# A four-layer convolution network on one core: layer 3's two row differences in one operation, on rows kept in blocks

## The chip, the cores and the metric

The kernel runs on one core of one Trainium2 chip. The metric is device time in microseconds (us) for one execution. The median of three runs of the kernel before is 2742.17 us (2739.24 to 2742.29).

## The reference

The input x is 16 images of 64 channels with 128 x 128 pixels, fp32. Four layers follow each other; each adds to x a function of the group-normalized x (`_gn`: 32 groups of 2 channels).

```
x = x + L0(gn(x))     # Gram matrix of the channels (64x64), applied to the image, then a 1x1 convolution
x = x + L1(gn(x))     # |Sobel x| + |Sobel y|, per channel
x = x + L2(gn(x))     # shift of a quarter of the channels to the left and of a quarter to the right, 3x3 convolution, bias
x = x + L3(gn(x))     # 3x3 convolution with w_bin, 1x1 convolution, batch norm over all images, leaky ReLU, clip to 0..255
```

Layer 3's batch normalization needs sums over all 16 images, so its result can only be finished and added to x when the last image is through.

## The kernel before

**Tiles.** 128 partitions hold 64 channels twice. An image is cut into chunks of R = 8 rows for each of the two sets of partitions, so NS = 8 chunks an image and 128 in all. One chunk of a tile is 128 partitions by 8 x 128 = 1024 elements. CP = 4 is half of the rows of a chunk.

**Order.** One loop over steps, with four quarters q = 0..3 in each, writes the whole order out by hand, for every engine; instructions of an engine stay in program order. In each quarter the stages are called in this order: parts of Front (layers 0 and 1) marked "first of", then Layer3, Layer2, Front, then Layer2's parts marked "last of 0" and "last of 3", then Gram (the Gram matrix of a later image), and then `tick()`, which advances the chains of small operations that make normalization coefficients. Front, Layer2 and Layer3 start at steps 15, 25 and 35, so for the most part a step works on one chunk of layer 1 of an image, one of layer 2 and one of layer 3 of earlier images. When the last chunk of one image and the first of the next meet in a stage, the step is called an image boundary here.

**A convolution by differences.** For two neighbouring output rows (even and odd), the 3x3 products are formed from one product that both share, on the odd rows (`shared`, into the PSUM tile `one`), and one of its own for each (`own`, into the halves of the PSUM tile `two`), on differences of rows: `difference(name, n, t)` (line 703) writes `diffs[name][:, n]`, with n = 0 for even minus odd row and n = 1 for the following even row minus odd row. The tile is `d3` for layer 3 and `d2` for layer 2. `twin(n)` copies a difference once more with its partition halves arranged differently, into qd; for layer 3 with two ScalarE copies, for layer 2 with two DMAs of GpSimd's queue. `own` needs the difference and its twin.

**Layer 3, chunk by chunk** (`Layer3.at`, line 955):

- q 0: twin(1) of the chunk; the shared product; the own product n = 0.
- q 1: the own product n = 1; ScalarE copies `one` with a bias into c; `prepare(i + 1)` (line 928) normalizes the next chunk's rows into a tile v3 of R + 1 = 9 rows in image order: one row from the chunk before, the four odd rows, the four even rows after them (line 942 and 944, in two ScalarE operations whose target takes every second row).
- q 2: VectorE adds `two` and c into y and sums it, which awaits the own products; then the next chunk's difference n = 0.
- q 3: twin(0) of the next chunk; its difference n = 1; ScalarE squares y and sums it.

**Layer 2** in q 0 adds the contributions of the two end columns of the image to the PSUM tile `two`, with one VectorE operation for the left and one for the right column (line 842), then forms x3 = two + c with its sum; then the difference n = 0 of `d2` follows and its twin; in "last of 3" the difference n = 1 and its twin. GpSimd scales the end columns of layer 2's v ahead of that (`keep0`, `keep1`, line 879).

**Front** puts most of VectorE's work: two operations in "first of 0", four in q 1, one in q 2 (called the gx product here, output u from xh) and one in q 3. In q 2 it stands behind layer 3's work on VectorE.

**The end.** Once the batch norm's coefficients are known, every part of y and of x3 is loaded back from memory, combined and stored as output; free tiles of all pools are used as buffers for that (`rest`, line 1033), those of v3 among them.

Of the kernel before, what the change touches and what calls it, by code (L numbers as in the profile page):

```python
# [10 lines left out]
F32 = mybir.dt.float32  # L11
# [5 lines left out]
P = 128  # L17
# [3 lines left out]
R = 8  # L21
NS = HH // R
EARLY = 3
CP = 4
# [84 lines left out]
def tile_kernel(ctx: ExitStack, tc: tile.TileContext, x, cw_h, w2_t, b2, wbin_t, w1_t, b1, gamma, beta, consts, out):  # L109
# [81 lines left out]

    wb = ring.tile([P, (R + 1) * W + 2], F32, tag="v2", name="wb", bufs=3)
    wb = wb[0:C, 0:9 * C].rearrange("p (y x c) -> p y x c", y=3, x=3)
    w1 = ring.tile([P, R + 1, W], F32, tag="v3", name="w1")[0:C, 0, 0:C]

    sp.dma_start(kc[:, 0:P], consts[:, 0:P])
    pool.dma_start(kc[:, P:K_END], consts[:, P:K_END])
# [499 lines left out]


    def by_parity(t):
        v = t[:, 0:R, :].rearrange("p (j s) w -> p s j w", s=2)  # L700
        return v[:, 0], v[:, 1]

    def difference(name, n, t, m=CP):


        even, odd = by_parity(t)
        after = t[:, 1:R + 1, :].rearrange("p (j s) w -> p s j w", s=2)[:, 1]
        dve.tensor_sub(diffs[name][:, n, 0:m, 1:1 + W], (after if n else even)[:, 0:m], odd[:, 0:m])

    def taps(o, p, wts, srcs, pad=0):  # L710

# [53 lines left out]
    class Layer2:  # L765
# [65 lines left out]
        def at(self, i, q):  # L831
            b = self.b
            closing = i + 1 == NS
            m = CP - 1 if closing else CP
            if q == 0:
                if i == NS:
                    chains.append(coefficients(self.st, self.done))
                if 1 <= i:
                    two = self.p.pop(i - 1)[0]

                    e = self.edges.pop(i - 1).rearrange("p t (m n) -> p t n m", n=2)
                    for side, w in ((0, 0), (1, W - 1)):
                        dve.tensor_add(two[:, :, :, w], two[:, :, :, w], e[:, side])
                    x3 = ring.tile([P, 2, CP, W], F32, tag="x3", name=f"x3_{b}_{i - 1}", bufs=NS + 2)
                    tiles3[b].append(x3)
                    dve.scalar_tensor_tensor(
                        x3.rearrange("p s j w -> p s (j w)"), two.rearrange("p s j w -> p s (j w)"), 1.0,
                        self.c.unsqueeze(1).to_broadcast([P, 2, CP * W]),
                        op0=ALU.mult, op1=ALU.add, accum_out=self.st[:, 0, i - 1:i],
                    )  # L850
                if 0 <= i < NS:
                    difference("d2", 0, self.v[i], m)
                    self.twin(0)
            if q == 1:
                if i == 0:

                    self.wi = stp.tile([P, 2, 3, P], F32, tag="wi", name=f"wi_{b}", bufs=1)
                    for n, base in ((0, w2[:, 2]), (1, wm)):
                        dve.scalar_tensor_tensor(
                            self.wi[:, n].rearrange("p k o -> p (k o)"), k("I3"), self.co[:, 2:3],  # L860
                            base.rearrange("p k o -> p (k o)"), op0=ALU.mult, op1=ALU.add,
                        )
                if -1 <= i < NS - 1:
                    if i == -1:
                        self.co = coefs2.pop(b)
                    t, f = self.v[i + 1], self.whole.pop(i + 1)
                    act.activation(f, f, AF.Identity, bias=self.co[:, 1:2], scale=self.co[:, 0:1])


                    e = stp.tile([P, 2, R], F32, tag="edges", name=f"edges_{b}_{i + 1}", bufs=3)  # L870
                    for side, at in ((0, 0), (1, W + 1)):
                        for rows, j in ((lo, 1), (hi, 0)):
                            n = at + j * W
                            pool.tensor_scalar_mul(
                                e[rows, side], f[rows, n:n + (R - 1) * W + 1:W], self.co[rows, 3 + side:4 + side]
                            )
                    self.edges[i + 1] = e

                    pool.tensor_scalar_mul(t[:, :, 0], t[:, :, 0], k("keep0"))
                    pool.tensor_scalar_mul(t[:, :, W - 1], t[:, :, W - 1], k("keep1"))  # L880
                if i + 2 < NS:
                    self.load(i + 2)
            if q == 2:
                if 0 <= i < NS:
                    t = self.v[i]
                    one = ps_one.tile([P, CP, W], F32, tag="one", name=f"one2_{b}_{i}")
                    two = ps_two.tile([P, 2, CP, W], F32, tag="two", name=f"two2_{b}_{i}")
                    self.p[i] = two, one
                    shared(one, self.wi[:, 0], t, m)
                    if closing:  # L890
                        small_product(one[:, m, :], w0, t[:, R, :])

                    both = self.wi[:, 1]
                    own(two[:, 1], 1, TO_SLOTS, w2, "d2", m, both)
                    if closing:

                        p = two[:, 1, m:CP]
                        issue([taps(0, p, [both], [t[:, R:R + 1, :]]), taps(1, p, [both], [t[:, R - 1:R, :]])])

                    self.c = ring.tile([P, CP * W], F32, tag="c2", name=f"c2_{b}_{i}", bufs=1)  # L900
                    act.activation(self.c, flat(one), AF.Identity, bias=self.co[:, 5:6])
                if 1 <= i < NS:
                    self.square(i - 1)
                if 1 <= i:
                    self.store(i - 1)
            if q == 3:
                if 0 <= i < NS:
                    t = self.v.pop(i)
                    two, one = self.p[i]
                    both = self.wi[:, 1]  # L910
                    own(two[:, 0], 0, TO_SLOTS, w2, "d2", m, both)
                    if closing:
                        p, srcs = two[:, 0, m:CP], [t[:, R - 2:R - 1, :], t[:, R - 1:R, :]]
                        issue([taps(0, p, [w2[:, 0], both], srcs), taps(1, p, [both, w2[:, 1]], srcs)])
            if q == "last of 0" and i == NS:
                self.square(i - 1)
            if q == "last of 3" and -1 <= i < NS - 1:
                difference("d2", 1, self.v[i + 1], CP if i + 2 < NS else CP - 1)
                self.twin(1)


    class Layer3:
# [4 lines left out]

        def prepare(self, i):
            b, tiles = self.b, tiles3[self.b]
            t = ring.tile([P, R + 1, W], F32, tag="v3", name=f"v3_{b}_{i}")  # L930
            self.v[i] = t

            def norm(dst, src, co):
                act.activation(dst, src, AF.Identity, bias=co[:, 1:2], scale=co[:, 0:1])

            if i == 0:
                self.co, self.edge = coefs3.pop(b)
                norm(t[:, 0, :], tiles[NS - 1][:, 1, CP - 1, :], self.edge["lower"])
            else:
                norm(t[:, 0, :], tiles[i - 1][:, 1, CP - 1, :], self.co)  # L940
            v = t[:, 1:R + 1, :].rearrange("p (n s) w -> p s n w", s=2)
            norm(v[:, 0], tiles[i][:, 0], self.co)
            m = CP if i + 1 < NS else CP - 1
            norm(v[:, 1, 0:m], tiles[i][:, 1, 0:m], self.co)
            if m < CP:
                norm(t[:, R, :], tiles[i][:, 1, m, :], self.edge["upper"])

        def twin(self, n):

# [5 lines left out]
        def at(self, i, q):  # L955
# [25 lines left out]
            if q == 2:  # L981
                if 0 <= i < NS:
                    y = ring.tile([P, 2, CP, W], F32, tag="y", name=f"y_{b}_{i}")
                    self.y[i] = y
                    two = self.p.pop(i)[0].rearrange("p s j w -> p s (j w)")
                    dve.scalar_tensor_tensor(
                        y.rearrange("p s j w -> p s (j w)"), two, 1.0,
                        self.c.unsqueeze(1).to_broadcast([P, 2, CP * W]),
                        op0=ALU.mult, op1=ALU.add, accum_out=bn_sum[:, n:n + 1],
                    )  # L990
                if i + 1 < NS:
                    difference("d3", 0, self.v[i + 1])
            if q == 3:
                if i + 1 < NS:
                    self.twin(0)
                    difference("d3", 1, self.v[i + 1])
                if 0 <= i < NS:
                    act.activation(
                        junk, self.y[i].rearrange("p s j w -> p (s j w)"), AF.Square,
                        accum_out=bn_sq[:, n:n + 1],  # L1000
                    )
# [104 lines left out]
        tick()  # L1106
    rest(ring, "x3", [2, CP, W], NS + 2, NS + 2 - 3 - (NS - 3))
    rest(ring, "y", [2, CP, W], 2)
    rest(ring, "v3", [R + 1, W], 2)
    while len(room) > 1:  # L1110
        fetch()

# [74 lines left out]
```

## Time and profile before

| | us |
|---|---|
| median of 3 runs | 2742.17 |
| the profiled execution, its own time | 2739.81 |
| its span, first to last instruction | 2738.0 |
| first y of layer 3 | 323.16 |
| last y of layer 3 | 2285.55 |
| last matmul of the network, about | 2285 |

The page gives busy time by engine, 40 slices of the span, and groups of instructions. Up to 300 us the pipeline fills; from there to 2050 all three layers run beside each other; to 2220 layers 2 and 3, to 2285 layer 3 alone; the rest is loading, finishing and storing. The mean granted TensorE clock is 0.899 over the span, and 1.00 in each stretch from 600 to 2250. Matmul ends are modelled, so that TensorE's idle time is better read from the distance of the starts of its instructions than from its busy share. All operations carry line 73, a helper that records the order, so groups are told apart by tile and shape.

### The profile page before, as it was taken

To read this page: it belongs to the slowest core of one execution; us is meant where nothing else is said; L and a number is where in the kernel's file an instruction comes from. 1 tells how busy PE (TensorE), PEld (TensorE's weight loads), DVE (VectorE), ACT (ScalarE), POOL (GpSimd) and SP (SyncE) were. 2 spreads that over 40 slices of the span, in tenths; PEclk is the share of its full clock that TensorE was granted. 3 is DMA by queue.
4 is the path that set the end of the run, shared out by engine and by line. 5 is a ranking of instruction groups with operands and counts; after the bars stand their busy time and mean duration, and the time that the engine had idled before them with its cause. 6 is when DMAs were issued, how large, how long until landed. Compare 5 with 4: busy or idle time off the path is not lost. (4 is left out here: it accounts for less than half of the span.)

```text
span 2738.0 us, 45982 instructions
## 1 busy us (share of the span) xinstructions
PE 2168.3 (79%) x14804; PEld 910.8 (33%) x14804; DVE 2190.3 (80%) x3623; ACT 2108.3 (77%) x3177; POOL 851.7 (31%) x1350
## 2 busy tenths in 40 slices
PE   6578899999999999999999999999999993000000
PEld 4234433434343434343434343333334641000000
DVE  4999999999999999999999999999996335333332
ACT  4766889898989898989899989898997677333332
POOL 2044424442434243333343434445444300000000
PEclk8689999999999999999999999999999997555555
DMA  8799878898888888888889787888887868999999
GB/s 209 200 232 235 224 198 238 217 240 220 236 231 234 226 228 226 228 224 234 224 226 239 211 201 201 204 211 207 220 204 187 226 188 308 419 420 420 420 420 385
DMA packets 693600, 685.95 MB, mean 251 GB/s; under 512 B 60096, under 2 KB 580448, under 8 KB 693360
## 3 DMA queue, kind: packets, MB, share of 16 engines
q1 hardware_dynamic: 668208, 613.83, 76.2%
q0 software_dynamic: 25152, 69.18, 10.0%
q8 instruction: 119, 1.95, 0.3%
q14 instruction: 121, 0.99, 0.1%
HBM read 346.23 MB, written 268.44 MB: 224 GB/s over the span
## 5 line engine op out<-in xcount | busy, mean ns | idle before, releaser
L73 PE MATMUL two<-d,w 128*64 128x508 f32 (+2 forms) x2560 | 855.5, 587 | 0.0
L73 PE MATMUL two<-d,wi 128*64 128x508 f32 (+3 forms) x1536 | 576.1, 578 | 0.0
L73 PE MATMUL two<-qd,pk 128*64 128x512 f32 (+1 forms) x1024 | 521.0, 590 | 27.9 <-DMA qd<-d 19.8
L73 POOL DMA_DIRECT2D qd<-d x512 | 270.8, 531 | 862.4 <-DVE d L73 284.5
L73 POOL TENSOR_SCALAR edges<-v,co 64x8 f32<-64x8 f32 x512 | 334.9, 654 | 352.5 <-ACT v L73 183.8
L73 DVE TENSOR_TENSOR d<-v 128x512 f32<-128x512 f32 (+1 forms) x512 | 346.0, 678 | 58.1 <-issue 30.8
L73 PEld LDWEIGHTS two<-d,w 128*64 128x64 f32 x2560 | 273.0, 136 | 325.1 <-issue 282.1
L73 PE MATMUL one<-v,w 128*64 128x508 f32 (+2 forms) x1600 | 364.6, 579 | 0.0
L73 PE MATMUL one<-v,wi 128*64 128x508 f32 (+3 forms) x1536 | 353.3, 591 | 2.5 <-issue 1.7
L73 ACT COPY qd<-d 64x512 f32<-64x512 f32 x512 | 315.5, 616 | 18.2 <-DVE d L73 12.2
L73 DVE SCALAR_TENSOR_TENSOR e<-e 128x1032 f32<-128x1032 f32 (+1 forms) x256 | 313.0, 1223 | 0.0
L73 ACT ACTIVATE xh<-po,co 128x128 f32<-128x128 f32 (+1 forms) x480 | 275.4, 623 | 26.1 <-PE po L73 22.4
L73 PEld LDWEIGHTS two<-d,wi 128*64 128x64 f32 x1536 | 178.8, 136 | 200.6 <-issue 178.8
L73 ACT ACTIVATE v<-x,co 128x512 f32<-128x512 f32 (+2 forms) x368 | 235.0, 705 | 0.0
L73 DVE SCALAR_TENSOR_TENSOR y<-two,c 128x1024 f32<-128x1024 f32 x128 | 156.0, 1219 | 94.6 <-ACT v L73 72.6
L73 POOL TENSOR_SCALAR v<-v,kc 128x9 f32<-128x9 f32 x256 | 217.9, 864 | 11.9
L73 PE MATMUL po<-x,abd 64*64 64x512 f32 (+1 forms) x1024 | 177.7, 640 | 46.5 <-ACT xh L73 43.1
L73 ACT ACTIVATE u<-u 128x1024 f32<-128x1024 f32 x128 | 135.4, 1058 | 75.1 <-DVE u L73 74.7
L73 PEld LDWEIGHTS two<-qd,pk 128*64 128x64 f32 x1024 | 130.8, 135 | 183.1 <-issue 86.4
L73 PEld LDWEIGHTS one<-v,w 128*64 128x64 f32 x1600 | 132.1, 136 | 171.7 <-issue 142.8
L73 DVE SCALAR_TENSOR_TENSOR u<-xh 128x1170 f32<-128x1170 f32 x128 | 175.4, 1370 | 3.8 <-ACT xh L73 3.8
L73 ACT ACTIVATE v<-v,co 128x1154 f32<-128x1154 f32 x128 | 172.1, 1345 | 6.0 <-DMA x_d<-x 3.3
(165 smaller groups left out, 3259.1 us busy)
## 6 DMA issues: line engine op xcount, KB each, us to landing
x<-in_x SPq DMA_DIRECT2D x256, 256.0 KB, 4.6
x_d<-u SPq DMA_DIRECT2D x512, 128.0 KB, 4.0
y_d<-y SPq DMA_DIRECT2D x512, 128.0 KB, 3.9
x_d<-x SPq DMA_DIRECT2D x496, 128.0 KB, 2.7
xr<-in_x SPq DMA_DIRECT2D x120, 512.0 KB, 6.2
qd<-d POOLq DMA_DIRECT2D x256, 130.0 KB, 3.4
qd<-d POOLq DMA_DIRECT2D x256, 129.8 KB, 3.9
v<-x_d SPq DMA_DIRECT2D x448, 72.1 KB, 3.0
```

Of the source, the lines that this page charges most:

```text
L73: return self.tc.keep_in_program_order(call(*args, **kwargs))
```

## The change

Rows of layer 3's tile v3 are kept in blocks, odd rows first and the even rows behind them, with one row more (R + 2) so that both blocks can be addressed with one pitch of five rows. One ScalarE operation normalizes both sets of four rows at once, except in an image's last chunk, whose last row has other coefficients. One VectorE operation in q 2 forms both differences: its first operand reads the even rows twice, from row 4 and from row 5 on, and its second repeats the odd rows. The difference in q 3 falls away. In layer 2, one VectorE operation adds both end columns.

```diff
     def by_parity(t):
+        if isinstance(t, tuple):
+            return t
         v = t[:, 0:R, :].rearrange("p (j s) w -> p s j w", s=2)
-        return v[:, 0], v[:, 1]
+        return v[:, 0], v[:, 1], t[:, 1:R + 1, :].rearrange("p (j s) w -> p s j w", s=2)[:, 1]
...
+    def both_differences(t):
+        first, second, _ = t
+        ap = [list(d) for d in first.ap]
+        both = bass.AP(first.tensor, first.offset, [ap[0], [W, 2], [W, CP], [1, W]])
+        dve.tensor_sub(
+            diffs["d3"][:, :, :, 1:1 + W], both, second.unsqueeze(1).to_broadcast([P, 2, CP, W])
+        )
...
-                    e = self.edges.pop(i - 1).rearrange("p t (m n) -> p t n m", n=2)
-                    for side, w in ((0, 0), (1, W - 1)):
-                        dve.tensor_add(two[:, :, :, w], two[:, :, :, w], e[:, side])
+                    e = self.edges.pop(i - 1).rearrange("p t (m n) -> p n m t", n=2)
+                    ends = two[:, :, :, 0:W:W - 1]
+                    dve.tensor_add(ends, ends, e)
...
-            t = ring.tile([P, R + 1, W], F32, tag="v3", name=f"v3_{b}_{i}")
-            self.v[i] = t
+            t = ring.tile([P, R + 2, W], F32, tag="v3", name=f"v3_{b}_{i}")
+            self.v[i] = t[:, CP:2 * CP], t[:, 0:CP], t[:, CP + 1:R + 1]
...
-                norm(t[:, 0, :], tiles[i - 1][:, 1, CP - 1, :], self.co)
-            v = t[:, 1:R + 1, :].rearrange("p (n s) w -> p s n w", s=2)
-            norm(v[:, 0], tiles[i][:, 0], self.co)
-            m = CP if i + 1 < NS else CP - 1
-            norm(v[:, 1, 0:m], tiles[i][:, 1, 0:m], self.co)
-            if m < CP:
-                norm(t[:, R, :], tiles[i][:, 1, m, :], self.edge["upper"])
+                norm(t[:, CP, :], tiles[i - 1][:, 1, CP - 1, :], self.co)
+            if i + 1 < NS:
+                v = t.rearrange("p (s n) w -> p s n w", s=2)[:, :, 0:CP]
+                norm(v.rearrange("p s n w -> p s (n w)"), tiles[i].rearrange("p s n w -> p s (n w)"), self.co)
+            else:
+                norm(t[:, 0:CP, :], tiles[i][:, 0], self.co)
+                norm(t[:, CP + 1:R, :], tiles[i][:, 1, 0:CP - 1], self.co)
+                norm(t[:, R, :], tiles[i][:, 1, CP - 1, :], self.edge["upper"])
...
                 if i + 1 < NS:
-                    difference("d3", 0, self.v[i + 1])
+                    both_differences(self.v[i + 1])
             if q == 3:
                 if i + 1 < NS:
                     self.twin(0)
-                    difference("d3", 1, self.v[i + 1])
```

More of the change, by code (lines that the diff above doesn't have):

```diff
@@ L193, in tile_kernel @@
     wb = wb[0:C, 0:9 * C].rearrange("p (y x c) -> p y x c", y=3, x=3)
-    w1 = ring.tile([P, R + 1, W], F32, tag="v3", name="w1")[0:C, 0, 0:C]
+    w1 = ring.tile([P, R + 2, W], F32, tag="v3", name="w1")[0:C, 0, 0:C]
     sp.dma_start(kc[:, 0:P], consts[:, 0:P])
@@ L699, in by_parity @@
     def by_parity(t):
+        if isinstance(t, tuple):
+            return t
         v = t[:, 0:R, :].rearrange("p (j s) w -> p s j w", s=2)
-        return v[:, 0], v[:, 1]
+        return v[:, 0], v[:, 1], t[:, 1:R + 1, :].rearrange("p (j s) w -> p s j w", s=2)[:, 1]
     def difference(name, n, t, m=CP):
-        even, odd = by_parity(t)
-        after = t[:, 1:R + 1, :].rearrange("p (j s) w -> p s j w", s=2)[:, 1]
+        even, odd, after = by_parity(t)
         dve.tensor_sub(diffs[name][:, n, 0:m, 1:1 + W], (after if n else even)[:, 0:m], odd[:, 0:m])
+    def both_differences(t):
[5 more added lines that the diff above has]
+        )
     def taps(o, p, wts, srcs, pad=0):
@@ L937, in prepare @@
                 self.co, self.edge = coefs3.pop(b)
-                norm(t[:, 0, :], tiles[NS - 1][:, 1, CP - 1, :], self.edge["lower"])
+                norm(t[:, CP, :], tiles[NS - 1][:, 1, CP - 1, :], self.edge["lower"])
             else:
-                norm(t[:, 0, :], tiles[i - 1][:, 1, CP - 1, :], self.co)
-            v = t[:, 1:R + 1, :].rearrange("p (n s) w -> p s n w", s=2)
-            norm(v[:, 0], tiles[i][:, 0], self.co)
-            m = CP if i + 1 < NS else CP - 1
-            norm(v[:, 1, 0:m], tiles[i][:, 1, 0:m], self.co)
-            if m < CP:
-                norm(t[:, R, :], tiles[i][:, 1, m, :], self.edge["upper"])
+                norm(t[:, CP, :], tiles[i - 1][:, 1, CP - 1, :], self.co)
[6 more added lines that the diff above has]
+                norm(t[:, R, :], tiles[i][:, 1, CP - 1, :], self.edge["upper"])
         def twin(self, n):
@@ L1108, in tile_kernel @@
     rest(ring, "y", [2, CP, W], 2)
-    rest(ring, "v3", [R + 1, W], 2)
+    rest(ring, "v3", [R + 2, W], 2)
     while len(room) > 1:
```

## Prediction

> **What bounds the kernel now.** I read the page first, then the windows view by stage, then the groups by shape, then the timelines of single engines over one step, and last the timeline around each place where TensorE lacks a tile.
>
> ```profile
> PE 2168.3 (79%) x14804; PEld 910.8 (33%) x14804; DVE 2190.3 (80%) x3623; ACT 2108.3 (77%) x3177; POOL 851.7 (31%) x1350
> ```
> ```profile
> 1200.00:1500.00 300.00, 296.90 (x2050) 121.57 (x2048) 285.58 (x495) 276.34 (x435) 109.11 (x184) 1.00 0.87 231
> 1800.00:2100.00 300.00, 297.79 (x1561) 108.37 (x1557) 281.83 (x431) 271.35 (x431) 143.20 (x204) 1.00 0.81 208
> 2200.00:2250.00 50.00, 48.79 (x252) 22.29 (x249) 17.95 (x39) 34.97 (x60) 0.00 (x0) 1.00 0.64 192
> 2300.00:2738.00 438.00, 0.00 (x0) 0.00 (x0) 147.38 (x122) 147.52 (x121) 0.00 (x0) 0.50 1.01 414
> ```
> The reader sees no single bound: in the long middle TensorE, VectorE and ScalarE are all over 90% busy; from 2200 on VectorE is nearly idle; from 2300 on DMA alone runs (share 1.01), and nothing of the change is there. So each stage must be asked which chain ends last.
>
> Price rows, by shape:
> ```profile
> L73 DVE TENSOR_TENSOR d<-v 128x512 f32<-128x512 f32 x480 | 328.2, 686 | 34.8 <-issue 12.4 <-ACT junk L73 9.3 <-POOL v L73 6.0
> L73 DVE TENSOR_TENSOR u<-u 128x1024 f32<-128x1024 f32 x128 | 156.0, 1219 | 0.0
> L73 DVE TENSOR_TENSOR two<-two,edges 128x8 f32<-128x8 f32 x256 | 43.6, 170 | 18.8 <-PE two L73 14.4
> L73 ACT ACTIVATE v<-x,co 128x512 f32<-128x512 f32 x240 | 182.3, 807 | 0.0
> L73 ACT ACTIVATE end_x<-end_x,sh,sc 128x1024 f32<-128x1024 f32 x39 | 47.9, 1237 | 84.2 <-DMA end_x<-y_d 84.2
> ```
> In the middle, TensorE is gapless over most of an image and loses time at an image boundary, where it waits for the difference copies qd (weight loads on TensorE, with the idle time before each):
> ```profile
> 1241.07 0.13 PEld L73 LDWEIGHTS two<-qd,pk 128*64 128x64 f32 x1 [1.33 <-DMA qd<-d]
> ...
> 1246.28 0.13 PEld L73 LDWEIGHTS two<-qd,pk 128*64 128x64 f32 x1 [0.75 <-ACT qd L73]
> ```
> A weight load has some 0.3 us of idle before it even in gapless work, so the first is about 1 us lost and the second 0.5. Two waits upstream set when ScalarE makes its copies there:
> ```profile
> 1218.18 0.17 DVE L73 TENSOR_REDUCE s<-st 128x2 f32<-128x16 f32 x1 [1.93 <-ACT junk L73]
> ...
> 1227.50 0.20 ACT L73 ACTIVATE sd<-nv 128x1 f32<-128x1 f32 x1 [0.84 <-DVE nv L73]
> ```
> In the tail, layer 3 alone (one chunk each 7.82 us), the chain is plain:
> ```profile
> 2246.43 1.22 DVE L73 SCALAR_TENSOR_TENSOR y<-two,c 128x1024 f32<-128x1024 f32 x1 [5.39 <-ACT v L73]
> 2247.59 0.08 DVE L73 DVE_READ_ACCUMULATOR y<-two,c 128x1 f32 x1
> 2247.59 1.29 DVE L73 TENSOR_TENSOR d<-v 128x512 f32<-128x512 f32 x2
> ...
> 2248.36 1.26 ACT L73 COPY qd<-d 64x512 f32<-64x512 f32 x2 [1.61 <-DVE d L73]
> ...
> 2249.68 0.64 PE L73 MATMUL two<-qd,pk 128*64 128x512 f32 x1
> ```
> Three rows of three engines: the first difference ends near 2248.27, ScalarE has waited 1.61 us for it, and TensorE starts qd 0.06 us after ScalarE's second copy ends (2249.62).
>
> [...] GpSimd's scaling of v took 3.00 us for two in the step from 1254.81, where VectorE then sat 0.22 us waiting for it.
>
> **The change, part by part.**
>
> *Differences.* Two 128x512 operations become one of 128x1024, 686+686 to 1219 ns. What VectorE really gives is the distance between starts in saturated stretches: 0.60 to 0.61 us for the 512 form, 1.14 for the 1024 form. Saving 0.07 us a chunk. The repeated second operand and overlapping first operand cost nothing extra by the same row (both fp32 SBUF, rows of 128 contiguous); bound from the other side, 0.1 us. What moves: everything behind it in quarter 2 (the step's gx product, the coefficient chains that tick there) comes 0.54 later; what is behind the old second difference in quarter 3 comes 0.07 earlier. The first copy (twin(0)) has to await 0.54 more. In the middle it has slack: from the difference's end to the copy I count 1.7 us or more in almost every chunk, ScalarE being behind. No wait on matmuls is added: y, just ahead, already awaits the products that read the second difference.
>
> *End columns.* Two operations of 170 ns that stand 0.20 apart (1214.01 to the next operation at 1214.42) become one of 16 elements: I take 0.20 for it, saving 0.2 us a chunk; bounds 0 (a slow strided PSUM form eats it) and 0.24.
>
> *Normalization.* For seven of eight chunks two 128x512 (starts 0.71 apart) become one 128x1024; the end_x row is the same form with two pointer operands, 1237 ns, 1.14 between starts. Saving 0.28 us of ScalarE, bounds 0.1 and 0.35. The extra row of v3 adds no instruction.
>
> [...]
>
> Now by stage, against the profiled execution (2739.81 us, span 2738.0).
>
> 1. Filling, 180 to 420 us. VectorE is 91 to 98% busy and bounds layer 2 before layer 3 joins: 9 chunks x 0.2 = 1.8, less where it idles anyway (2.90 us before d at 205.07): 1.4 saved. Four crowded steps after that: 0.6. Total -2.
> 2. Nine image boundaries with the Gram products running (430 to 1500). In the one shown, ScalarE is saturated from 1191.16 (a wait for TensorE) to the sum of squares that lets s start: one normalization lies between, so s comes 0.28 earlier. From s VectorE is saturated to nv, with the longer difference in between: 0.54 - 0.28 = 0.26 later at sd. ScalarE is then saturated up to the copies at 1246.28 and 1248.78, with one normalization between (1235.37): 0.26 - 0.28 = -0.02. These copies release TensorE, and after them it is gapless until the next boundary. So the stall fed by DMA shrinks, but those fed by ScalarE take its place: 9 x -0.02, about 0.
> 3. Four boundaries without them (1619 to 2010). Here ScalarE has slack (2.15 us idle before u at 1885.13) and VectorE lags: where its timeline has no gap, y follows y after 14.55 us, and TensorE, gapless, takes 14.83 from one layer 2 chunk to the next. It carries its lag into the boundary, where some 2 us of TensorE are lost (about 0.9 in the first). Six steps x 0.27 = 1.6 less lag, less the 0.54 once at sd: about 1.1 each, 4 in all. Total -4.4.
> 4. Layers 2 and 3 alone, 2034 to 2186: steps of 13.68 us are TensorE's own work; layer 2's products lie between y and the copy. 0.
> 5. The tail: seven chunks, each with the chain above. 7 x 0.54 = +3.8. The later copies in the chain move along, and faster normalization is off this chain.
>
> Sum: -2 + 0 - 4.4 + 3.8 = -2.6 us: 2737.2 for the profiled execution, and from the median 2742.17 (which stands 2.4 above that execution) **2739.6 us**. About 0.2% (5.5 us) is what a measurement of this kernel can tell from no change, so the likeliest case counts as the same.
>
> **Rivals.**
>
> *Faster by about 10 us.* If sd isn't what holds the nine boundaries (for instance because the coefficient chain runs in VectorE's gain of earlier steps too), each gains 0.27 x 3 steps = 0.8, so another 7: 2732.4. For it: all three engines are near full there, and both VectorE and ScalarE are relieved. Against: ScalarE's 0.84 us wait for nv is in the trace, with the longer operation ahead of it. Chance 0.28.
>
> *Slower, by the place of the longer operation.* It stands ahead of gx, of nv and of GpSimd's scalings. If GpSimd is held so that the layer 2 difference in "last of 3" waits 0.3 us more a step, VectorE's gain of 0.27 is gone (stage 3: 0), and if ScalarE doesn't make good the 0.54 at sd, nine boundaries cost 0.54 each, 4.9. With -2 and +3.8: +6.7, 2748.8. It decides once the added hold passes the 0.28 us of ScalarE and 0.27 of VectorE. For it: the 0.22 us waits on GpSimd's v that exist already, 18 of them. [...] Chance 0.22.
>
> *Hidden anyway.* TensorE is the bound in 1 to 4, only the tail shows: +3.8, 2746.0. For it: TensorE's 297 of 300 us. Against: the gaps at qd. Chance 0.12. (Of the same kind is that the change doesn't do what it says, with a new operation at half rate: 1.2 us more a chunk on a saturated VectorE would be tens of us; the row of the same size speaks against it.)
>
> **Numbers.** Forecast 0.38, faster 0.28, slower 0.22, hidden 0.12. The forecast's own range, 2735 to 2744 from the bounds of its parts. The range for 8 in 10 reaches to both outer cases: 2731 to 2749. Faster by over 0.2% (below 2736.7): the first rival and a little of the forecast, 0.33. Slower (above 2747.7): most of the second rival and a little of the third, 0.23. Within: 0.44.
>
> **What would show it.** One d row of 128x1024 near 1219 ns (x128), one of 128x16 for the ends near 0.2 us, a v row of 128x1024 near 1237 (x112). Tail steps of 8.36 us instead of 7.82. The wait of sd for nv about 1.1 us instead of 0.84, and TensorE's gaps at the two ScalarE copies about as before; at the boundaries from 1619 on, smaller gaps. VectorE's wait for GpSimd's v still 0.22 us, not half a us. I am wrong if the d row is far from 1219, if the tail steps keep 7.82, or if steps of 14.55 us get longer.

## The result, and the profile after

The change takes 2736.45 us (median of 20 runs, 2733.72 to 2740.86) where the kernel before takes 2740.89 (20 runs beside it): a ratio of 0.9985 [0.9978, 0.9992]. That is a gain of 4.4 us, or 0.15%: clear of zero, but within the 0.2% that the prediction counts as no change. The span of the profiled execution goes from 2738.0 to 2735.2 us. The forecast was 2739.6 us, and -2.6 us by its sum.

The sum holds better than its terms. From the starts of y, step by step, in the two profiles:

| stage | forecast | measured |
|---|---|---|
| 1 filling (to the first y, and one image more) | -2 | -0.54 and -0.25 |
| 2 nine boundaries with Gram products | 0 | -4.2 (-0.24 to -0.86 each) |
| 3 boundaries without them | -4.4 for four | -3.1 for three (-1.34, -0.87, -0.88) |
| 4 layers 2 and 3 alone, with the fourth of those boundaries | 0 | -0.04 |
| 5 tail, its first two chunks apart | +3.8 | +4.0 and +1.0 |
| from the last y to the end | 0 | +0.25 |

Busy time on the page of the changed kernel; VectorE and ScalarE have 256 and 112 instructions fewer:

```profile
PE 2170.7 (79%) x14804; PEld 907.0 (33%) x14804; DVE 2166.7 (79%) x3367; ACT 2077.5 (76%) x3065; POOL 874.2 (32%) x1350
```

By stretches, in the columns used above (sum, TensorE, weight loads, VectorE, ScalarE, GpSimd, clock, DMA share, GB/s):

```profile
1200.00:1500.00 300.00, 296.15 (x2046) 121.28 (x2046) 283.25 (x457) 272.05 (x417) 114.65 (x185) 1.00 0.88 233
1800.00:2100.00 300.00, 299.67 (x1569) 111.40 (x1567) 276.26 (x392) 266.85 (x416) 148.61 (x209) 1.00 0.81 209
```

The reader sees that all three are still busy for 89% or more of both stretches. From 1800 VectorE and ScalarE each have about 5 us less to do in 300, but the changed kernel is some 6 to 8 us ahead there, so that its stretch holds more of the stage without layer 1. Over the same two images, 243.48 us long before (1763.09:2006.57) and 242.31 after (1756.33:1998.64), VectorE goes from 239.51 to 237.56 us, ScalarE from 225.93 to 222.84, and TensorE, with 240.76 and 241.36, gets closer to full.

The groups by shape show that every operation costs what its row was taken for:

```profile
L73 DVE TENSOR_TENSOR d<-v 128x1024 f32<-128x1024 f32 x128 | 157.1, 1228 | 0.0
L73 DVE TENSOR_TENSOR d<-v 128x512 f32<-128x512 f32 x224 | 154.1, 688 | 39.1 <-issue 17.1 <-ACT junk L73 7.7 <-POOL v L73 3.3
L73 ACT ACTIVATE v<-x,co 128x1024 f32<-128x1024 f32 x112 | 138.3, 1235 | 0.0
L73 DVE TENSOR_TENSOR two<-two,edges 128x16 f32<-128x16 f32 x128 | 22.5, 175 | 14.4 <-PE two L73 14.4
```

The overlapping and the repeated operand add 9 ns at most (1228 beside 1219 of the plain form), the strided PSUM form of 16 elements takes 175 ns where 8 took 170, and the idle time of d that GpSimd ends went from 6.0 us to 3.3.

At the boundary that was shown, the waits of the small operations s (VectorE's timeline) and sd (ScalarE's) in the changed kernel:

```profile
1214.50 0.17 DVE L73 TENSOR_REDUCE s<-st 128x2 f32<-128x16 f32 x1 [1.94 <-ACT junk L73]
```
```profile
1224.35 0.20 ACT L73 ACTIVATE sd<-nv 128x1 f32<-128x1 f32 x1 [1.37 <-DVE nv L73]
```

Each kernel's times are counted from one event, the c<-one that ended ScalarE's wait of 4.04 and 4.33 us for TensorE (it starts at 1191.16 before, 1187.74 after). s then comes at 27.03 before and 26.77 after, sd at 36.34 and 36.61: 0.26 earlier and 0.27 later, as worked out. The wait itself grew by 0.53 to 1.37, not to 1.1, since ScalarE arrives 0.26 earlier as well as nv 0.27 later. But the copies, and TensorE behind them, come earlier than forecast. Weight loads of the changed kernel, from TensorE's timeline:

```profile
1238.15 0.13 PEld L73 LDWEIGHTS two<-qd,pk 128*64 128x64 f32 x1 [1.55 <-DMA qd<-d]
...
1242.55 0.19 PEld L73 LDWEIGHTS two<-qd,pk 128*64 128x64 f32 x2
...
1245.03 0.13 PEld L73 LDWEIGHTS two<-qd,pk 128*64 128x64 f32 x1 [0.58 <-ACT qd L73]
```

From the same event the DMA-fed load comes at 50.41 us (49.91 before), the first copy-fed one at 54.81 (55.12), the second at 57.29 (57.62). So the stall fed by DMA did not shrink here: it grew from 1.33 to 1.55 us, though its transfer was issued 0.54 us earlier; the transfer took 5.2 us to land where it had taken 4.0. Over all nine boundaries it does shrink, at six of them: it was 0.92 to 2.96 us, and is 0.97 to 1.84 at four, 0.68 and 0.41 at two, and too short to count (under 0.33) at three. But it trades with the stall behind ScalarE's first copy: before, the two add up to 2.07 or 2.08 us at seven of the nine, and after, the first copy's load waits about 0.8 us at the five where the DMA's is short, and has no wait to show here. What moves TensorE is that the copies themselves come earlier.

Why, is seen in the kernel before. Its VectorE, then its ScalarE, just ahead of those copies:

```profile
1237.98 1.22 DVE L73 TENSOR_TENSOR u<-u 128x1024 f32<-128x1024 f32 x1
1239.12 1.22 DVE L73 SCALAR_TENSOR_TENSOR e<-e 128x1024 f32<-128x1024 f32 x1
```
```profile
1238.02 1.17 ACT L73 COPY xw<-xr 128x1024 f32<-128x1024 f32 x1
1239.23 1.06 ACT L73 ACTIVATE u<-u 128x1024 f32<-128x1024 f32 x1
1240.37 1.06 ACT L73 ACTIVATE e<-e 128x1024 f32<-128x1024 f32 x1
```

Two ScalarE operations start 0.03 us after VectorE's products end (1239.20 and 1240.34). Neither carries a bracket with a wait, so the stretch had passed for saturated. But ScalarE starts u 1.21 us after the operation ahead of it, and e 1.14 after u. In the changed kernel, where VectorE starts this e 47.42 us after the common event instead of 47.96, the same two distances are 1.05 and 0.96:

```profile
1234.61 1.21 ACT L73 COPY xw<-xr 128x1024 f32<-128x1024 f32 x1
1235.66 1.08 ACT L73 ACTIVATE u<-u 128x1024 f32<-128x1024 f32 x1
1236.62 1.07 ACT L73 ACTIVATE e<-e 128x1024 f32<-128x1024 f32 x1
```

So ScalarE had waited 0.16 and 0.18 us. With sd 0.27 later, the normalization 0.28 shorter and these 0.34 us gone, the copies should come 0.35 earlier, and the loads show 0.31 and 0.33. It is the same at all nine boundaries with Gram products: from sd to the first of the copies it is 17.48 or 17.49 us before and 16.87 to 16.89 after; ScalarE starts u 0.03 us after VectorE's u ends before, and 0.42 to 0.44 after it now.

### The profile page after: what moved, and what is told of

The parts are those of the page before. It is cut to its first block, busy times and chain, and to the rows that moved or that the text cites. A ratio compares the mean times of both kernels' runs of the same rounds, so it can differ in the third digit from the quotient of the medians.

```text
span 2735.2 us, 45604 instructions
## 1 busy us (share of the span) xinstructions
PE 2170.7 (79%) x14804; PEld 907.0 (33%) x14804; DVE 2166.7 (79%) x3367; ACT 2077.5 (76%) x3065; POOL 874.2 (32%) x1350
## 5 line engine op out<-in xcount | busy, mean ns | idle before, releaser
L73 POOL TENSOR_SCALAR edges<-v,co 64x8 f32<-64x8 f32 x512 | 366.2, 715 | 352.9 <-ACT v L73 264.4
L73 DVE TENSOR_TENSOR d<-v 128x512 f32<-128x512 f32 (+2 forms) x384 | 329.1, 857 | 64.8 <-issue 37.7
L73 DVE SCALAR_TENSOR_TENSOR y<-two,c 128x1024 f32<-128x1024 f32 x128 | 156.0, 1219 | 102.6 <-issue 47.1
L73 POOL TENSOR_SCALAR v<-v,kc 128x9 f32<-128x9 f32 x256 | 208.9, 830 | 12.0
L73 ACT ACTIVATE v<-x,co 128x1024 f32<-128x1024 f32 (+3 forms) x256 | 203.8, 847 | 0.0
L73 ACT ACTIVATE c<-one,co 128x512 f32<-128x512 f32 x128 | 86.9, 679 | 123.6 <-PE one L73 119.9
```

Of the source, the lines that this page charges most:

```text
L73: return self.tc.keep_in_program_order(call(*args, **kwargs))
```

## Experiments

The times below are medians beside runs of the kernel before on the same chip; ratios have their 95% interval. "Stages" are differences of y's starts to the kernel before, as in the table, each from one profile.

**The three parts one by one.** ends_alone has only the change of the end columns, norm_alone only blocks and one normalization (differences stay two, in q 2 and q 3), diff_alone the blocks and one difference, with two normalizations and two end columns:

ends_alone, against the kernel before:

```diff
...
-                    for side, w in ((0, 0), (1, W - 1)):
-                        dve.tensor_add(two[:, :, :, w], two[:, :, :, w], e[:, side])
+                    ends = two[:, :, :, 0:W:W - 1]
+                    dve.tensor_add(ends, ends, e)
```

norm_alone, against the changed kernel (the end columns by two operations too; a condition that always holds is left out):

```diff
                 if i + 1 < NS:
-                    both_differences(self.v[i + 1])
+                    difference("d3", 0, self.v[i + 1])
             if q == 3:
                 if i + 1 < NS:
                     self.twin(0)
+                    difference("d3", 1, self.v[i + 1])
```

diff_alone, against the changed kernel (the end columns likewise):

```diff
-                norm(v.rearrange("p s n w -> p s (n w)"), tiles[i].rearrange("p s n w -> p s (n w)"), self.co)
+                for s in range(2):
+                    norm(v[:, s], tiles[i][:, s], self.co)
```

> The kernel before with the one operation for both end columns alone. Theory (VectorE's lag at image boundaries costs TensorE time, 0.2 us a chunk is taken off it): the boundaries without Gram products lose less, about 1 us each of four, the nine with Gram products little, the tail stays at 7.82 us a chunk; 2 to 5 us faster in all. Rival (ScalarE's time is what counts, VectorE has room): within 1 us of before.

Measured: 2732.80 us, 0.9969 [0.9959, 0.9980]. Stages: -0.08 to -0.51 at each boundary with Gram products, -1.63, -1.04, -1.04 at those without, 0.0 in the tail; a step of saturated VectorE takes 14.35 us (from 14.55). That is 8 us by the medians, more than the 2 to 5 expected. The first y comes 3.3 us earlier, more than this part explains; other profiles of this study differ by 2 to 3 us there too, so filling isn't read finer than that.

> Rows in blocks and the one normalization, but two differences of 512 elements in their old places, and two operations for the end columns. Theory (at the nine boundaries with Gram products ScalarE's chain sets when TensorE gets its copies): about 0.3 us less at each, nothing at the other four, tail steps at 7.82 us; 2 to 4 us faster. Rival (VectorE's time is what counts): within 1 us of before.

Measured: 2738.72 us, 0.9992 [0.9984, 1.0000]. Stages: about -0.3 at each boundary with Gram products, 0 (+0.03 to +0.08) without, 0 in the tail. The gain of 2.3 us by the medians is as expected. It comes ahead of sd, which is 0.25 to 0.30 us earlier. From sd to the copies it takes 17.49 or 17.50 us, as before, since ScalarE, done sooner, waits longer for VectorE's u, which it again follows at 0.03 or 0.04 us.

> Rows in blocks and the one operation for both differences, with two normalizations and two operations for the end columns. Theory (the longer operation stands in the chain from y to the first copy in the tail, and ahead of nv at the boundaries): tail steps of 8.36 us, 5 us in all there, and 0 to 0.3 us more at each boundary; 4 to 8 us slower than before. Rival (the loss in the tail is due to the new rows or the wider normalization, not to the longer operation): within 1 us of before plus nothing in the tail.

Measured: 2749.35 us, 1.0033 [1.0020, 1.0045]. Stages: about +0.3 at most boundaries with Gram products, +0.28 to +0.65 without, +3.7 in the tail and +1.0 at its first two chunks; the saturated step grew to some 14.68 us. That is 8.3 us slower, the upper end of what was expected. So the part that names the change, the merged difference, loses in the sum of every stage from the boundaries to the tail, also where VectorE is saturated and one operation was to save 0.07 us.

**Why the merged difference costs time.** VectorE in the kernel before, at the gx product and its reader (the product that reads u, in q 3), then in the changed kernel:

```profile
1902.46 1.30 DVE L73 SCALAR_TENSOR_TENSOR u<-xh,co,u 128x1024 f32<-128x1024 f32 x1
1903.67 0.68 DVE L73 TENSOR_TENSOR d<-v 128x512 f32<-128x512 f32 x1
1904.27 1.27 DVE L73 SCALAR_TENSOR_TENSOR u<-e,co,u 128x1024 f32<-128x1024 f32 x1
```
```profile
1894.58 1.24 DVE L73 TENSOR_TENSOR d<-v 128x1024 f32<-128x1024 f32 x1
1895.74 1.29 DVE L73 SCALAR_TENSOR_TENSOR u<-xh,co,u 128x1024 f32<-128x1024 f32 x1
1897.15 1.29 DVE L73 SCALAR_TENSOR_TENSOR u<-e,co,u 128x1024 f32<-128x1024 f32 x1
```

The difference that went away stood between a product and the operation that reads it. Now the reader starts 1.41 us after the product, where the difference had started 1.21 after it and left the reader 0.60 later. From the start of the first difference to that of the reader it is 0.62 + 1.21 + 0.60 = 2.43 us before (the 0.62 from 1901.84, the difference n = 0) and 1.16 + 1.41 = 2.57 after. The merged operation costs 0.14 us in such a step instead of saving 0.07. With the 0.2 of the end columns, the step shrinks by some 0.06 to 14.47 or 14.50, not to 14.28. The same trace has steps in which small operations of the coefficient chains stand between the product and its reader, in both kernels. There, in 45 of 48 such steps, the reader comes 0.05 to 0.08 us earlier after y than before, as forecast, and where VectorE is saturated these steps shrink by 0.25 to 0.28 us. In the two traces two starts lie 0.60 us apart at 512 elements and 1.14 at 1024, so that two operations in place of one take 0.06 us more, and the distance behind the gx product is 0.2 us longer where the next operation reads its output: 1.38 to 1.42 us to its reader, 1.18 to 1.23 to any other operation.

The run filler puts a small operation between the two, a memset of 32 elements that nobody reads:

```diff
             if q == 3:
+                dve.memset(scratch, 0.0)
                 dve.scalar_tensor_tensor(
                     gx, gy, self.co[:, 3:4], gx, op0=ALU.add, op1=ALU.add, accum_out=self.st[:, 0, i:i + 1]
                 )
```

> The changed kernel with one small VectorE operation on a scratch tile (a memset of 32 elements) between the gx product and the product that reads its result. Theory (the 1.41 us are the wait for the gx product's result to be written): the small operation stands in that wait and costs at most 0.05 us a chunk, 1.41 becomes 1.41 to 1.46, the time that of the changed kernel within 2 us. Rival (the gx product itself is slowed, by the longer operation ahead or by GpSimd): the small operation adds 0.1 us or more a chunk, steps of 14.50 become 14.60 or more.

```profile
1899.12 1.29 DVE L73 SCALAR_TENSOR_TENSOR u<-xh,co,u 128x1024 f32<-128x1024 f32 x1
1900.37 0.09 DVE L73 MEMSET scratch<- 128x32 f32 x1
1900.53 1.29 DVE L73 SCALAR_TENSOR_TENSOR u<-e,co,u 128x1024 f32<-128x1024 f32 x1
```

1.25 + 0.16 = 1.41 us: the added operation is free and the step keeps its length. So the reader starts 1.41 us after the product with the memset between them as without it, which fits a wait for the product's result. The time as a whole missed the expectation: 2742.94 us, 1.0006 [0.9997, 1.0014], 6.5 us above the changed kernel by the medians. In the profiles, the boundaries with Gram products take 0.24 us more than in the changed kernel on average (from -0.2 to +0.9), and the time after the last y 1.8 us more. Why is open; the memset itself doesn't lengthen the saturated step.

late_diff moves the merged operation there, to the head of q 3; the last image, and the step ahead of its first coefficients, have two differences:

```diff
                 if i + 1 < NS:
-                    both_differences(self.v[i + 1])
+                    if b == B - 1 or (b == B - 2 and i == NS - 2):
+                        difference("d3", 0, self.v[i + 1])
             if q == 3:
                 if i + 1 < NS:
+                    if not (b == B - 1 or (b == B - 2 and i == NS - 2)):
+                        both_differences(self.v[i + 1])
                     self.twin(0)
...
```

> The changed kernel with the one operation for both differences moved from quarter 2 to the head of quarter 3, so that it stands between the gx product and its reader and behind nv; in the tail (the last image, and the last chunk of the image before) two operations as before. Theory: the distance gx to reader is covered, saturated steps are 14.28 us, sd waits for nv no longer than before, tail 7.82; 10 to 13 us less than before, ratio 0.996. Rival (the first copy now waits for the difference, which ends 1.75 us later than in the kernel before, where the slack was 1.7 and more): ScalarE idles ahead of qd, and it is no better than the version with two operations throughout.

Measured: 2730.07 us, 0.9958 [0.9945, 0.9971], as expected, but the step isn't:

```profile
1894.12 1.28 DVE L73 SCALAR_TENSOR_TENSOR u<-xh,co,u 128x1024 f32<-128x1024 f32 x1
1895.31 1.22 DVE L73 TENSOR_TENSOR d<-v 128x1024 f32<-128x1024 f32 x1
1896.45 1.28 DVE L73 SCALAR_TENSOR_TENSOR u<-e,co,u 128x1024 f32<-128x1024 f32 x1
...
1897.96 0.69 DVE L73 TENSOR_TENSOR d<-v 128x512 f32<-128x512 f32 x1 [0.22 <-POOL v L73]
```

The 1.41 is gone (1.19 and 1.14), so the dependence is covered. In its place layer 2's difference now waits 0.22 us for GpSimd's scaling of v, and the step is 14.57 us; in the images without Gram products the first step, without that wait, takes 14.27 or 14.28 as expected. That is the wait for GpSimd that the slower rival names, though it comes with another order, not with the change as made.

**The parts of the change without the merged difference.** ends_norm is the changed kernel with two differences, as before (a condition that always holds is left out):

```diff
-                    both_differences(self.v[i + 1])
+                    difference("d3", 0, self.v[i + 1])
...
                     self.twin(0)
+                    difference("d3", 1, self.v[i + 1])
```

> The changed kernel with the two differences as two operations of 512 elements in quarters 2 and 3 throughout (rows in blocks, one normalization, one operation for the end columns). Theory (the one difference costs time everywhere: the gx product is now followed directly by its reader, 1.41 us from start to start where it was 1.22, and the tail loses 5 us): steps without other work of 14.35 us, tail of 7.82 us; about 10 us less than before, ratio 0.9964. Rival (the parts only overlap, what end columns and normalization gain is the same time): no better than the end columns alone, 0.9969.

Measured: 2729.11 us, 0.9952 [0.9938, 0.9967], a little better than expected; about -0.5 at boundaries with Gram products, -1.59, -1.37, -1.35 without, 0 in the tail, a saturated step of 14.34 us. It is 7.3 us below the changed kernel by the medians (9 us by the two ratios): that is what the merged difference costs, of which the tail with its entry is 5.

tail_split takes the merged difference away in the last image alone, with the same condition in q 3:

```diff
+                    if b == B - 1:
+                        difference("d3", 0, self.v[i + 1])
+                    else:
                         both_differences(self.v[i + 1])
```

> The changed kernel, but in the last image the two differences stand as two operations of 512 elements in quarters 2 and 3, as before. Theory: tail steps of 7.82 us again, and 5 us less than the changed kernel, so about 2731.5 where before is 2740.9 (ratio 0.9966). Rival (block rows or wide normalization make the tail longer): steps of 8.36 us stay, and the ratio is that of the changed kernel, 0.9985.

Measured: 2732.25 us, 0.9969 [0.9957, 0.9982], as expected. Tail steps are 7.82 us again, and the seven chunks differ from the kernel before by -0.03. The +0.9 at the tail's entry stays: it falls in the last but one image's chunk 6, which still has the merged operation, ahead of a chain of coefficients.

**The merged difference at the coefficient chain.** boundary_split has two differences only in the step before an image's first chunk (`i == -1`); split_at_6 only in the step of chunk 6, which is the one ahead of nv. The latter, with the same condition in q 3:

```diff
-                    both_differences(self.v[i + 1])
+                    if i == NS - 2:
+                        difference("d3", 0, self.v[i + 1])
+                    else:
+                        both_differences(self.v[i + 1])
```

> The changed kernel, but for the first chunk of each image the two differences stand as two operations, as before. Theory (at an image boundary the longer operation ahead of nv delays ScalarE's copies): sd waits 0.84 us for nv instead of 1.37, and each of the nine boundaries with Gram products gives 0.3 us more than in the changed kernel, the other four 0.5; some 4 to 5 us less than the changed kernel. Rival (the wait is hidden behind ScalarE's other work): within 1 us of the changed kernel.

Measured: 2735.37 us, 0.9978 [0.9969, 0.9987], and sd still waits 1.37 us. The edit stood in the wrong step: the coefficients of the next image's layer 2 come while layer 3 is at chunk 6. It says nothing about sd.

> The changed kernel, but in the step in which chunk 6 of an image is in layer 3 (there the coefficients of the next image's layer 2 are made, and sd waits for nv) the two differences stand as two operations. Theory: sd waits 0.84 us instead of 1.37, each of the nine boundaries with Gram products takes 0.2 to 0.3 us less than in the changed kernel, the other four 0.4, and the step at the entry of the tail is 0.5 shorter: 4 to 5 us less than the changed kernel, 2732. Rival (the copies there are held by ScalarE's other work, not by sd): only the tail's entry, within 1 us of the changed kernel.

Measured: 2734.60 us, 0.9979 [0.9970, 0.9988]. The wait of sd is 0.84 us again, yet seven of the boundaries with Gram products gain only 0.09 to 0.22 us each over the changed kernel, two lose 0.5 and 0.9 in this profile, and those without gain nothing; the +0.9 at the tail's entry is gone. I expected 4 to 5 us less than the changed kernel and got 2. So sd, half a us earlier, isn't what sets these boundaries. From sd to the copies it takes 17.28 or 17.29 us, 0.41 more than in the changed kernel: VectorE's u comes no earlier than there, and ScalarE again starts its own u 0.03 us after it. That leaves some 0.13 of the 0.54 us.

**The tail.** ends_norm_square also moves, in the last image, ScalarE's sum of squares of y behind twin(1) of the next step; square_late_all does so for every image. The first, against the changed kernel, without the two differences and without the square's removal from q 3:

```diff
                 self.twin(1)
+                if b == B - 1 and i > 0:
+                    self.square(i - 1)
```

> Two differences throughout, with the one operation for end columns and the one normalization, and in the last image ScalarE's square of y behind twin(1) instead of ahead of it. Theory (in the tail the loop is y, difference, twin(0), square, twin(1), own product, y): the square's 1.15 us leave the loop until TensorE's own 6.83 us bound it, tail steps of 6.8 to 6.95 instead of 7.82, 6 to 7 us less than without this move: 2722.5. Rival (TensorE's own order of products makes 7.82): no change against the version without the move.

Measured: 2729.68 us, 0.9962 [0.9949, 0.9975], as ends_norm. Tail steps stay 7.82 us. My theory that the square ahead of the copies is part of the loop fell: y comes at 2244.60 and 2252.42, though the square no longer stands between the copies. What is left as a loop is y, the difference n = 0 behind it, twin(0), the own products, and y again.

> As the last one, with the square of y behind twin(1) in all images. Theory (at boundaries twin(1) is what TensorE waits for, and it comes 1.15 us earlier): 0.3 to 0.8 us less at each of thirteen boundaries, 4 to 8 us less than with the move in the last image alone: 2716 to 2719. Rival (twin(1) isn't alone in holding TensorE there, the copy by DMA and twin(0) end as late): within 1.5 us of the last one.

Measured: 2729.59 us, 0.9960 [0.9947, 0.9973]; nothing gained over the last one, so the theory for the boundaries fell too.

diff_first tests that loop: ends_norm, and in the last image the difference n = 0 stands ahead of y on VectorE, not behind it. Against ends_norm:

```diff
             if q == 2:
+                if b == B - 1 and i + 1 < NS:
+                    difference("d3", 0, self.v[i + 1])
                 if 0 <= i < NS:
...
-                if i + 1 < NS:
+                if i + 1 < NS and b < B - 1:
                     difference("d3", 0, self.v[i + 1])
```

> Two differences throughout, with the one operation for end columns and the one normalization; in the last image the difference n = 0 of the next chunk stands ahead of y on VectorE instead of behind it. Theory (in the tail the loop is y, difference n = 0, twin(0), the own products behind it, y, and the square isn't in it): the difference needs only the rows and the end of the own product n = 0, so y's 1.15 us and part of the rest leave the loop until TensorE's own 6.83 us bound it; tail steps of 6.85 to 7.1 instead of 7.82, 5 to 7 us less than without this move. Rival (the difference waits for the last own product in any case, both halves lying in one tile): 7.1 to 7.82 with a gain of at most 1.15 us a chunk less what TensorE then waits, or none.

Measured: 2723.66 us, 0.9936 [0.9922, 0.9950], the fastest of all, some 13 us below the changed kernel (2736.45) and 5 below ends_norm by the medians. Its tail in VectorE's timeline, then in ScalarE's:

```profile
2241.78 0.69 DVE L73 TENSOR_TENSOR d<-v 128x512 f32<-128x512 f32 x1 [4.17 <-ACT v L73]
2242.60 1.23 DVE L73 SCALAR_TENSOR_TENSOR y<-two,c 128x1024 f32<-128x1024 f32 x1
...
2249.43 1.23 DVE L73 SCALAR_TENSOR_TENSOR y<-two,c 128x1024 f32<-128x1024 f32 x1
```
```profile
2242.50 1.26 ACT L73 COPY qd<-d 64x512 f32<-64x512 f32 x2 [0.76 <-DVE d L73]
```

The copy no longer comes after y: it starts 0.10 us ahead of it. y follows y after 6.83 or 6.84 us instead of 7.82, six times, and after 6.89 at the last, which makes the 6.87 us measured for the last seven chunks against the kernel before. TensorE has no gap of over 0.3 us before a weight load there: it is now the bound. The loop had been the tail's bound, and one difference, moved, is worth more than the whole change.

## Why the prediction was right, point by point

**Filling, -2.** Measured -0.8 in the profiles. As profiles of this stage differ by 2 to 3 us among themselves, no run here tests the term.

**Nine boundaries, 0.** The upper half of the step holds: s 0.26 earlier, sd 0.27 later. The step that failed is the next one, "ScalarE is then saturated up to the copies". It was not: it followed VectorE's products u and e at 0.03 us, in waits too short to carry a bracket. VectorE reaches them 0.54 us earlier, so the copies come 0.3 us earlier, not 0.02, and nine boundaries give 4.2 us, not nothing. The waits are in the traces of all nine, and norm_alone and split_at_6 bear them out: in each, ScalarE gains on VectorE ahead of u and loses the gain waiting for it. The 0.3 us make up some 3 of the 4.2 us; the rest lies in three boundaries with 0.48 to 0.86, and in one of them the kernel before waits 2.96 us for a DMA in this profile. Why the others gain more is open.

**Boundaries without Gram products, -4.4.** Measured -3.1 for three and nothing for the fourth. The mis-sized term is the 0.27 us of VectorE a step. Where the product and its reader stand next to each other it is 0.06, with 0.2 from the end columns as taken and +0.14 from the merged difference where -0.07 was taken; where coefficient operations stand between them it is 0.25 to 0.28, as taken. The gain is the sum of such steps all through an image rather than a lag made good at its boundary: in the image with -1.34, four steps with coefficient operations give 0.26 to 0.28 each and four without 0.05 to 0.07. In the next two images only two steps have such operations, five give 0.05 to 0.12 and one gives nothing: -0.87 and -0.88. The parts by themselves don't always add up. In the image with -1.34 they do (-1.63 and +0.28). In the next two ends_alone brings -1.04, as one step grows by 0.08 where the others shrink by 0.2: layer 2's difference there waits 0.22 us for GpSimd, as it does neither before nor in the changed kernel. diff_alone costs 0.6 there.

**Layers 2 and 3 alone, 0.** As forecast (-0.04).

**Tail, +3.8.** The chain is the one named, and its steps are 8.36 us as forecast:

```profile
2240.68 1.23 DVE L73 SCALAR_TENSOR_TENSOR y<-two,c 128x1024 f32<-128x1024 f32 x1 [5.99 <-issue]
...
2249.04 1.22 DVE L73 SCALAR_TENSOR_TENSOR y<-two,c 128x1024 f32<-128x1024 f32 x1 [5.99 <-issue]
```
```profile
2243.14 1.26 ACT L73 COPY qd<-d 64x512 f32<-64x512 f32 x2 [2.42 <-DVE d L73]
```

The copies wait 2.42 us instead of 1.61. Left out was the chunk at the tail's entry, where the coefficients of the last image pass behind the longer operation: +0.9, gone in split_at_6. tail_split shows the seven steps to be worth 4 us by themselves.

**The waits for GpSimd, 0.** That they would stay as they were was my estimate. They did not grow, as forecast, but fell. VectorE's waits for GpSimd's v in front of layer 2's difference fell from 18 (6.0 us; 15 of them are the 0.22 us that the prediction names, three 0.47 to 1.24) to 4 (3.3 us), all four before 500 us. The other runs with the merged difference in q 2 have 4 to 6 of them; those with two differences have 18 or 19, but ends_alone has 28 (8.8 us); late_diff has 36 (11.1 us). So the waits go with the merged operation in q 2; how is not shown, and neither is a delay of GpSimd's scaling by a longer VectorE operation.

**The rivals.** The faster one had the right sign at the nine boundaries and twice the size (0.8 each, measured 0.24 to 0.86 and on average 0.47); it fails as a whole by what the merged difference takes back. The slower one's 0.54 at sd is in the trace as a wait longer by 0.53, but ScalarE makes it good. "Hidden anyway" fell: -7.3 us came at the boundaries. So the tail was understood, but that the total came out right owes much to luck, to errors that balance: one gain was missed, another taken too large, and a loss at the tail's entry left out.

## What to carry to other kernels

Before two operations are merged, look at what the one that goes away stood between: here a difference of 0.60 us between the gx product and its reader added only 0.4 to the distance of their starts (1.81 us), and merged into an operation ahead of both it left 1.41 with nothing in between. In a loop where one engine's result comes round again, ask of every operation in it whether it must stand behind the one that closes the loop; here, in the tail, moving one difference ahead of y gave 7 us in the profile, and merging it with the other cost 4. A stretch in which an engine's operations start a few hundredths of a us after those of another engine end, as here twice at 0.03 us, need not be saturated, though no wait is printed: ScalarE had waited 0.16 and 0.18 us there.

## What was not expected of the hardware

Two VectorE operations of 1024 fp32 elements, with two SBUF inputs each, start 1.14 us apart in most places when independent, and an operation that does not read the gx product's output starts 1.18 to 1.23 behind it. The gx product and the operation that reads its output start 1.38 to 1.42 apart when nothing stands between them. An independent operation in between cost less than its own length: 0.16 us of a memset went in at no cost (1.25 + 0.16 = 1.41), and 0.60 us of a difference added only 0.4 (1.81). What the memset's run lost elsewhere stays unexplained.
